# Self-attention of a channel-attention layer: diagonal chunk pairs computed on and above the diagonal only, the rest mirrored like other pairs

## The chip, the cores and the metric

The kernel runs on one core of a Trainium2 chip, and the metric is the device time of one execution in microseconds (us). An execution was profiled besides; its span runs from its first to its last instruction. The engines are called by their names in the profile: PE (TensorE), ACT (ScalarE), DVE (VectorE), POOL (GpSimd) and SP (SyncE, which here only issues DMAs).

## The reference, cut to what matters

`x` has shape 4 x 32 x 128 x 128, all in float32. Layer 0 regroups each image to 128 channels at 64 x 64 = 4096 tokens and lets the 4096 tokens of each image attend to one another, by cosine similarity of their 128 channels:

```python
q = xs.reshape(B, C * R * R, hw)                       # 4 x 128 x 4096
energy = jnp.einsum('bci,bcj->bij', q, q)              # 4096 x 4096, symmetric
d = jnp.sqrt(jnp.diagonal(energy, axis1=1, axis2=2))
energy = energy / (d[:, :, None] * d[:, None, :])
attn = jax.nn.softmax(energy, axis=-1)
out = jnp.einsum('bcj,bij->bci', q, attn)
out = gamma * out + xs
```

Layer 1 takes the result as tokens of 128 features: a layer norm, a linear attention without softmax over 8 heads, a residual; then a layer norm, a router over 8 experts of which the two best are mixed, and a residual.

What matters here is that the energy, and so its exponential before the division by the row sums, is symmetric: block (i, j) of exp(energy) is the transpose of block (j, i).

## The kernel before, in words

**Tiling of layer 0.** The 4096 tokens of an image are cut into 8 chunks of 512 (`NCH`), and each chunk into 4 blocks of 128 (`NJ`). `qn[i]` is chunk i of the normalised q (128 channels x 512 tokens), `qT[i]` the same chunk of q with tokens on the partitions. `attend` (line 207) loops over the chunks i (a *row* below, lines 213 to 251) and in it over the chunk pairs (i, jc) with jc up to i (line 221); a pair has 4 steps, j = 0 to 3. Thus an image has 36 pairs, of which 8 are diagonal (jc = i), and 144 steps. Only pairs on and below the diagonal of chunks are computed; the mirrored ones come by transposition.

**A step** (lines 225 to 240): PE computes 128 x 512 energies into the PSUM tile `pe` (line 228); ACT takes the exponential into `pr`, with its row sum into `sums` (line 230); PE adds the previous step's values to `po`, the output of chunk i (`values`, line 219, one step late); DVE transposes the 32 x 32 squares of `pr` into `F`, when the pair is not diagonal (line 234).

**The end of a pair that is not diagonal** (lines 241 to 247): the squares are in place but still have to go to the partitions of their mirrored block. Sixteen DMAs, from SBUF to SBUF, one for each of 4 x 4 groups of 32 partitions, take `F` to `G` (line 246). All are issued by SP. Then `transposed_share` (line 189) is put on the list `late`: 4 units, of which each is a matmul of `G` into `pg` (line 193) and an ACT copy of `G` that only serves its row sum (line 198); the last unit adds `pg` to `o[jc]`, the output of chunk jc (line 204). A unit is taken from the list at a step, not before 4 steps after the pair's end (`LAG`), one share after the other.

**A diagonal pair** computes all of its 4 x 4 blocks directly, and has no `F`, no `G` and no share.

**Buffers** that set how far one engine may run ahead of another: `pe` 2, `pr` 6, `F` 2, `G` 3, `po` 1, `pg` 1.

**Side work.** `prep` (line 144) loads a part of an image (`xx`), transposes and normalises it. `layer1` (line 259) carries layer 1 of an image; it loads `x` again as `T`, divides by the row sums (`den`, line 283), adds on POOL (line 335), and so on until the output DMAs (line 518). The loop at the end (lines 532 to 553) spreads these over the steps of `attend`: image 0 has only `prep` and the weights beside it; images 1 to 3 have layer 1 of the image before, from step 9 to step 138, and `prep` of the next near their end. Layer 1 of the last image runs alone at the end.

**What sets the order.** The loops give the order of the program. A scheduler in the kernel's framework then orders each engine's instructions by this order and by when it expects their inputs to be ready, so that for instance the four `pg` matmuls of a share may stand together, and places the waits. Each engine, and SP's queue, works through its own list in order. SP's list holds the loads of `xx` and `T` (line 141), the sixteen `G<-F` DMAs of each pair and the output DMAs.

Of the kernel before, what the change touches and what calls it, by code (L numbers as in the profile page):

```python
# [9 lines left out]
F32 = mybir.dt.float32  # L10
BF16 = mybir.dt.bfloat16
AF = mybir.ActivationFunctionType
ALU = mybir.AluOpType
# [5 lines left out]
def kernel(  # L19
# [10 lines left out]
    expert_b: bass.AP,  # L30
    out: bass.AP,
):

# [16 lines left out]
    nc = tc.nc  # L52
    P = 128
    B, C, H, W = x.shape
    N = (H // 2) * (W // 2)
    NB = N // P
    CH = 512
    NCH = N // CH
    NJ = CH // P
    HW2 = W // 2  # L60
    KT = 32
    S = 32
# [12 lines left out]
    work = ctx.enter_context(tc.tile_pool(name="work", bufs=2))  # L75
    stat = ctx.enter_context(tc.tile_pool(name="stat", bufs=2))
# [111 lines left out]

    def transposed_share(b, st, i, jc, G):

        pg = ps_g.tile([P, CH], F32, tag="pg", name=f"pg_{b}_{i}_{jc}")
        for ib in range(NJ):
            nc.tensor.matmul(  # L193
                pg, st["qT"][i][:, ib, :], G[:, ib].rearrange("p a j -> p (a j)"),
                start=(ib == 0), stop=(ib == NJ - 1),
            )
            junk = work.tile([P, CH], BF16, tag="junk", name=f"junk_{b}_{i}_{jc}_{ib}")
            nc.scalar.activation(  # L198
                junk, G[:, ib].rearrange("p a j -> p (a j)"), AF.Copy,
                accum_out=st["sums"][:, NJ * i + ib, jc : jc + 1],  # L200
            )
            if ib == NJ - 1:
                o = st["o"][jc].rearrange("p (j a c) -> p a j c", a=4, c=S)
                nc.vector.tensor_tensor(o, o, pg.rearrange("p (a j c) -> p a j c", a=4, c=S), ALU.add)  # L204
            yield "done" if ib == NJ - 1 else None

    def attend(b, st):

        qT, qn = st.setdefault("qT", {}), st.setdefault("qn", {})
        st["sums"] = sums = stat.tile([P, NB, NCH], F32, tag="sums", name=f"sums_{b}")  # L210
        st["o"] = []

        for i in range(NCH):
            po = ps_o.tile([P, CH], F32, tag="po", name=f"po_{b}_{i}")
            pend = None

            def values(pend, i=i, po=po):
                pr, t = pend
                nc.tensor.matmul(po, qT[t // NJ][:, t % NJ, :], pr, start=(t == 0), stop=(t == NJ * (i + 1) - 1))  # L219

            for jc in range(i + 1):
                off = jc < i
                if off:
                    F = fpool.tile([P, CH // S, NJ, S], F32, tag="F", name=f"F_{b}_{i}_{jc}")
                for j in range(NJ):
                    t = NJ * jc + j
                    pe = ps_e.tile([P, CH], F32, tag="pe", name=f"pe_{b}_{i}_{t}")
                    nc.tensor.matmul(pe, qn[jc][:, ts(j, P)], qn[i], start=True, stop=True)  # L228
                    pr = ppool.tile([P, CH], F32, tag="pr", name=f"pr_{b}_{i}_{t}")
                    nc.scalar.activation(pr, pe, AF.Exp, accum_out=sums[:, t, i : i + 1])  # L230
                    if pend is not None:
                        values(pend)
                    if off:
                        nc.vector.transpose(F[:, :, j, :], pr)  # L234
                    pend = (pr, t)
                    clock[0] += 1
                    if late and late[0][0] <= clock[0]:
                        if next(late[0][1], "done") == "done":
                            late.pop(0)
                    yield  # L240
                if off:
                    G = gpool.tile([P, NJ, 4, P], F32, tag="G", name=f"G_{b}_{i}_{jc}")
                    blocks = F.rearrange("p (ib q) j c -> p q ib (j c)", q=4)
                    for a in range(4):
                        for q in range(4):
                            nc.sync.dma_start(G[ts(q, S), :, a, :], blocks[ts(a, S), q])  # L246
                    late.append((clock[0] + LAG, transposed_share(b, st, i, jc, G)))
            values(pend)
            o = opool.tile([P, CH], F32, tag="o", name=f"o_{b}_{i}")
            nc.vector.tensor_copy(o, po)  # L250
            st["o"].append(o)
# [280 lines left out]
    for b in range(B):  # L532
        streams = []
        if b == 0:
            for kc, begin, end in ((1, 0, 8), (2, 10, 26), (3, 30, 60)):
                streams.append((prep(0, kc, states[0]), begin, end, 9))
            streams.append((setup_weights(), 60, 70, 3))
        else:
            p = states[b - 1]
            work_left = layer1(b - 1, p, False)  # L540
            streams.append((work_left, 9, 138, SIDE))
        if b + 1 < B:
            for kc, at in enumerate((96, 121, 128, 134)):
                streams.append((prep(b + 1, kc, states[b + 1]), at, at + 9, 9))
        done = [0] * len(streams)
        for t, _ in enumerate(attend(b, states[b])):
            for n, (steps, begin, end, count) in enumerate(streams):
                while t >= begin and done[n] * (end - begin) < (t + 1 - begin) * count:
                    next(steps, None)
                    done[n] += 1  # L550
        for steps, *_ in streams:
            for _ in steps:
                pass
    finish_late()
    last = states[B - 1]
# [40 lines left out]
```

## Time and profile before

| | us |
|---|---|
| three runs | 1920.04, 1922.54, 1923.35 |
| median | 1922.54 |
| the profiled execution's own time | 1923.41 |
| its span | 1921.4 |
| first `pe` matmul of image 0, 1, 2, 3, from the span's start | 19.7, 381.4, 852.0, 1306.7 |
| last `G<-F` issue | 1753.0 |

A line of the costliest groups reads: line, engine, operation, out<-in by the program's names, shapes, count, then busy time and mean ns of one, then the idle time of the engine before these and what ended most of it. A float32 matmul shows as two records. A line of the timeline reads: start, duration, engine, line, operation, tiles, count of like instructions in a row. SP's records are the times for which the issue of a DMA held its queue. A line of SP's waits reads: who waited for whom, us in total, times, longest. Image 0 lasts from 19.7 to about 381 and has little side work; in images 1 to 3 the first rows, 0 to 2, have little as well.

### The profile page before, as it was taken

The numbers are of one execution on the slowest core, as the hardware profiler recorded it, in microseconds if no ns is written. First come the engines' busy times: TensorE is split into PE (matmuls) and PEld (weight loads), VectorE is DVE, ScalarE is ACT, GpSimd is POOL, SyncE is SP. The second block draws the span as 40 slices with busy tenths as digits, with TensorE's granted clock in tenths as the row PEclk, the third lists the DMA queues.
The fourth block names the chain that finished last, engine by engine and source line by source line (L and its number), as shares of the span: only waits on it lengthen the run. The fifth ranks groups of instructions, "written<-read, shape, count | busy, mean of one in ns | idle before, by whom it ended". The sixth has DMA issues, their size and how long they took to land.

```text
span 1921.4 us, 20402 instructions
## 1 busy us (share of the span) xinstructions
PE 1845.2 (96%) x5320; PEld 897.6 (47%) x5320; DVE 880.0 (46%) x2029; ACT 959.0 (50%) x2925; POOL 293.0 (15%) x275
## 2 busy tenths in 40 slices
PE   6999999999999999999999999999999999996787
PEld 3444444444555444444555444444555444443643
DVE  3333333444335454645344454653534544444456
ACT  2444444445564454554665545454556454543544
POOL 0000000012000121212010122220200012211235
PEclk9999999999999999999999999999999999998879
DMA  5333343341333232344232233334222323234001
GB/s 118 77 88 75 88 102 92 97 88 47 74 78 85 64 84 74 82 96 88 65 89 70 68 81 79 80 85 94 65 62 70 86 66 86 63 87 93 1 12 33
DMA packets 314274, 145.63 MB, mean 76 GB/s; under 512 B 32528, under 2 KB 314160, under 8 KB 314160
## 3 DMA queue, kind: packets, MB, share of 16 engines
q1 hardware_dynamic: 310528, 142.73, 31.3%
q10 hardware_dynamic: 3632, 1.60, 0.4%
q8 instruction: 44, 0.72, 0.2%
q14 instruction: 70, 0.57, 0.1%
HBM read 18.38 MB, written 8.39 MB: 14 GB/s over the span
## 4 chain that ended last, share of the span: by engine, by line
PE 85%; DVE 5%; POOL 4%; ACT 3%; DMA 2%; SPq 1%; issue 1%; ACTq 0%; POOLq 0%; DVEq 0%
PE po L219 24%; PE pe L228 23%; PE pg L193 19%; PE py L505 5%; PE py L498 5%; PE pl L419 2%; PE pat L400 1%; PE pbe L488 1%; DVE df L327 1%; POOL T L335 1%; ACT xn L310 1%; PE ptn L179 1%; ACT tmp L507 1%; PE pgram L353 1%; SPq L246 1%
## 5 line engine op out<-in xcount | busy, mean ns | idle before, releaser
L230 ACT ACTIVATE pr<-pe 128x512 f32<-128x512 f32 x576 | 343.7, 597 | 600.7 <-PE pe L228 593.2
L219 PE MATMUL po<-pr,qT 128*128 128x512 f32 x1152 | 589.9, 595 | 3.2 <-ACT pr L230 1.9
L234 DVE STREAM_TRANSPOSE F<-pr 128x512 f32<-128x512 f32 x448 | 308.6, 703 | 337.4 <-ACT pr L230 304.5
L228 PE MATMUL pe<-qn,qn 128*128 128x512 f32 x896 | 456.6, 594 | 0.2
L193 PE MATMUL pg<-G,qT 128*128 128x512 f32 x896 | 422.6, 597 | 2.6 <-DMA G<-F 2.6
L219 PEld LDWEIGHTS po<-pr,qT 128*128 128x128 f32 x1152 | 213.9, 190 | 275.4 <-issue 232.5
L198 ACT ACTIVATE junk<-G 128x512 bf16<-128x512 f32 x448 | 276.2, 624 | 3.7 <-DMA G<-F 3.7
L193 PEld LDWEIGHTS pg<-G,qT 128*128 128x128 f32 x896 | 170.6, 192 | 214.0 <-issue 209.7
L507 ACT ACTIVATE tmp<-py,gate 128x128 f32<-128x128 f32 x512 | 146.4, 370 | 180.3 <-PE py L505 156.8
L228 PEld LDWEIGHTS pe<-qn,qn 128*128 128x128 f32 x896 | 160.9, 191 | 159.6 <-issue 157.8
L500 DVE SCALAR_TENSOR_TENSOR acc<-py,gate,acc 128x128 f32<-128x128 f32 x512 | 175.5, 349 | 107.6 <-PE py L498 94.2
L511 POOL TENSOR_TENSOR tmp<-tmp 128x512 f32<-128x512 f32 x64 | 81.6, 1275 | 620.3 <-ACT tmp L507 620.3
L204 DVE TENSOR_TENSOR o<-o,pg 128x512 f32<-128x512 f32 x112 | 76.7, 685 | 213.9 <-PE pg L193 213.0
L505 PE MATMUL py<-ew_sb,xn 128*128 128x512 f32 x256 | 133.1, 606 | 4.4 <-ACT tmp L507 4.4
L498 PE MATMUL py<-ew_sb,xn 128*128 128x512 f32 x256 | 130.5, 595 | 2.6 <-DVE acc L500 2.3
L228 PE MATMUL pe<-qn 128*128 128x512 f32 x256 | 131.6, 597 | 0.0
L230 ACT ACTIVATION_READ_ACCUMULATOR pr<-pe 128x1 f32 x576 | 114.2, 198 | 0.0
L105 POOL TENSOR_TENSOR rn<-ss,neg_half 128x8 f32<-128x8 f32 x16 | 26.3, 1642 | 463.8 <-DVE ss L169 463.8
L198 ACT ACTIVATION_READ_ACCUMULATOR junk<-G 128x1 f32 x448 | 87.9, 196 | 0.0
L505 PEld LDWEIGHTS py<-ew_sb,xn 128*128 128x128 f32 x256 | 48.5, 193 | 67.0 <-issue 42.2
L498 PEld LDWEIGHTS py<-ew_sb,xn 128*128 128x128 f32 x256 | 47.6, 191 | 63.1 <-issue 38.9
L310 ACT ACTIVATE xn<-T,nb_a,rs_a 128x128 f32<-128x128 f32 x128 | 51.2, 480 | 40.9 <-DVE nb_a L306 40.8
(99 smaller groups left out, 1213.3 us busy)
## 6 DMA issues: line engine op xcount, KB each, us to landing
G<-F SPq DMA_DIRECT2D x1792, 64.0 KB, 2.1
xx<-in_x_dram SPq DMA_DIRECT2D x64, 128.0 KB, 3.0
T<-in_x_dram SPq DMA_DIRECT2D x16, 512.0 KB, 5.7
out_dram<-acc SPq DMA_DIRECT2D x128, 64.0 KB, 1.8
ew_sb<-in_L_ffn_expert_w_dram ACTq DMA_DIRECT2D x1, 512.0 KB, 5.5
raw_w<-in_L_attn_Wv_dram ACTq DMA_DIRECT2D x1, 512.0 KB
raw_w<-in_L_attn_Wk_dram ACTq DMA_DIRECT2D x1, 256.0 KB
raw_w<-in_L_attn_Wq_dram ACTq DMA_DIRECT2D x1, 256.0 KB
```

Of the source, the lines that this page charges most:

```text
L193: nc.tensor.matmul(pg, st["qT"][i][:, ib, :], G[:, ib].rearrange("p a j -> p (a j)"), start=(ib == 0), stop=(ib == NJ - 1),)
L198: nc.scalar.activation(junk, G[:, ib].rearrange("p a j -> p (a j)"), AF.Copy, accum_out=st["sums"][:, NJ * i + ib, jc : jc + 1],)
L204: nc.vector.tensor_tensor(o, o, pg.rearrange("p (a j c) -> p a j c", a=4, c=S), ALU.add)
L219: nc.tensor.matmul(po, qT[t // NJ][:, t % NJ, :], pr, start=(t == 0), stop=(t == NJ * (i + 1) - 1))
L228: nc.tensor.matmul(pe, qn[jc][:, ts(j, P)], qn[i], start=True, stop=True)
L230: nc.scalar.activation(pr, pe, AF.Exp, accum_out=sums[:, t, i : i + 1])
L234: nc.vector.transpose(F[:, :, j, :], pr)
L498: nc.tensor.matmul(py, xn[:, k, :], ew_sb[:, 0:4, :], start=True, stop=True)
L500: nc.vector.scalar_tensor_tensor(acc[:, j, :], py[:, ts(e, D)], gate[:, k, e : e + 1], acc[:, j, :], ALU.mult, ALU.add)
L505: nc.tensor.matmul(py, xn[:, k, :], ew_sb[:, 4:8, :], start=True, stop=True)
L507: nc.scalar.activation(tmp[:, jk, e, :], py[:, ts(e, D)], AF.Copy, scale=gate[:, k, 4 + e : 5 + e])
L511: nc.gpsimd.tensor_tensor(tmp[:, :, 0:2], tmp[:, :, 0:2], tmp[:, :, 2:4], ALU.add)
```

## The change

In a diagonal pair, step j computes only the columns from block j on, `c0 = 128 j`: pe and po have 512, 384, 256 and 128 columns, and so has the exponential. The six blocks below the diagonal are mirrored from those above as in other pairs: DVE transposes the columns above the diagonal of steps 0 to 2 into `F` (384, 384 and 256 columns; one block on the diagonal is taken along), POOL sets one block of `F` to zero that the DMAs read and nobody writes, SP issues 16 DMAs with 3 rows of 96 values for each of 32 partitions, where other pairs have 4 rows of 128, and a share of 3 units follows, with `pg` matmuls of 384, 256 and 128 columns. Its row sums go to a ninth column of `sums`, which POOL sets to zero once an image. The last diagonal pair of the last image stays as it was (`full`), so that 31 of the 32 are changed. A few blank lines are left out of the diff.

```diff
@@ -188,26 +189,32 @@
 
     def transposed_share(b, st, i, jc, G):
 
+
+
         pg = ps_g.tile([P, CH], F32, tag="pg", name=f"pg_{b}_{i}_{jc}")
-        for ib in range(NJ):
-            nc.tensor.matmul(
-                pg, st["qT"][i][:, ib, :], G[:, ib].rearrange("p a j -> p (a j)"),
-                start=(ib == 0), stop=(ib == NJ - 1),
+        pgv = pg.rearrange("p (a f) -> p a f", a=4)
+        blocks = [(ib, P) for ib in range(NJ)] if jc < i else [(ib, S * ib) for ib in range(NJ - 1, 0, -1)]
+        for n, (ib, w) in enumerate(blocks):
+            last = n == len(blocks) - 1
+            src = G[:, ib, :, :w]
+            nc.tensor.matmul(pgv[:, :, :w], st["qT"][i][:, ib, :], src, start=(n == 0), stop=last)
+            junk = work.tile([P, 4, P], BF16, tag="junk", name=f"junk_{b}_{i}_{jc}_{ib}")
+            col = jc if jc < i else NCH
+            nc.scalar.activation(
+                junk[:, :, :w], src, AF.Copy, accum_out=st["sums"][:, NJ * i + ib, col : col + 1]
             )
-            junk = work.tile([P, CH], BF16, tag="junk", name=f"junk_{b}_{i}_{jc}_{ib}")
-            nc.scalar.activation(
-                junk, G[:, ib].rearrange("p a j -> p (a j)"), AF.Copy,
-                accum_out=st["sums"][:, NJ * i + ib, jc : jc + 1],
-            )
-            if ib == NJ - 1:
-                o = st["o"][jc].rearrange("p (j a c) -> p a j c", a=4, c=S)
-                nc.vector.tensor_tensor(o, o, pg.rearrange("p (a j c) -> p a j c", a=4, c=S), ALU.add)
-            yield "done" if ib == NJ - 1 else None
+            if last:
+                nj = blocks[0][1] // S
+                o = st["o"][jc].rearrange("p (j a c) -> p a j c", a=4, c=S)[:, :, :nj]
+                add = pg.rearrange("p (a j c) -> p a j c", a=4, c=S)[:, :, :nj]
+                nc.vector.tensor_tensor(o, o, add, ALU.add)
+            yield "done" if last else None
 
     def attend(b, st):
 
         qT, qn = st.setdefault("qT", {}), st.setdefault("qn", {})
-        st["sums"] = sums = stat.tile([P, NB, NCH], F32, tag="sums", name=f"sums_{b}")
+        st["sums"] = sums = stat.tile([P, NB, NCH + 1], F32, tag="sums", name=f"sums_{b}")
+        nc.gpsimd.memset(sums[:, :, NCH:], 0.0)
         st["o"] = []
 
         for i in range(NCH):
@@ -215,35 +222,46 @@
             pend = None
 
             def values(pend, i=i, po=po):
-                pr, t = pend
-                nc.tensor.matmul(po, qT[t // NJ][:, t % NJ, :], pr, start=(t == 0), stop=(t == NJ * (i + 1) - 1))
+                pr, t, c0 = pend
+                nc.tensor.matmul(
+                    po[:, c0:], qT[t // NJ][:, t % NJ, :], pr[:, c0:], start=(t == 0), stop=(t == NJ * (i + 1) - 1)
+                )
 
             for jc in range(i + 1):
-                off = jc < i
-                if off:
+                within = jc == i
+                full = within and b == B - 1 and i == NCH - 1
+                if not full:
                     F = fpool.tile([P, CH // S, NJ, S], F32, tag="F", name=f"F_{b}_{i}_{jc}")
                 for j in range(NJ):
                     t = NJ * jc + j
+                    c0 = P * j if within and not full else 0
                     pe = ps_e.tile([P, CH], F32, tag="pe", name=f"pe_{b}_{i}_{t}")
-                    nc.tensor.matmul(pe, qn[jc][:, ts(j, P)], qn[i], start=True, stop=True)
+                    nc.tensor.matmul(pe[:, c0:], qn[jc][:, ts(j, P)], qn[i][:, c0:], start=True, stop=True)
                     pr = ppool.tile([P, CH], F32, tag="pr", name=f"pr_{b}_{i}_{t}")
-                    nc.scalar.activation(pr, pe, AF.Exp, accum_out=sums[:, t, i : i + 1])
+                    nc.scalar.activation(pr[:, c0:], pe[:, c0:], AF.Exp, accum_out=sums[:, t, i : i + 1])
                     if pend is not None:
                         values(pend)
-                    if off:
+                    if not within:
                         nc.vector.transpose(F[:, :, j, :], pr)
-                    pend = (pr, t)
+                    elif not full and j < NJ - 1:
+                        c1 = max(c0, P)
+                        nc.vector.transpose(F[:, c1 // S :, j, :], pr[:, c1:])
+                    pend = (pr, t, c0)
                     clock[0] += 1
                     if late and late[0][0] <= clock[0]:
                         if next(late[0][1], "done") == "done":
                             late.pop(0)
                     yield
-                if off:
+                if not full:
                     G = gpool.tile([P, NJ, 4, P], F32, tag="G", name=f"G_{b}_{i}_{jc}")
                     blocks = F.rearrange("p (ib q) j c -> p q ib (j c)", q=4)
+                    ib0, w = 0, P
+                    if within:
+                        nc.gpsimd.memset(F[:, 4:8, 2, :], 0.0)
+                        ib0, w = 1, 3 * S
                     for a in range(4):
                         for q in range(4):
-                            nc.sync.dma_start(G[ts(q, S), :, a, :], blocks[ts(a, S), q])
+                            nc.sync.dma_start(G[ts(q, S), ib0:, a, :w], blocks[ts(a, S), q, ib0:, :w])
                     late.append((clock[0] + LAG, transposed_share(b, st, i, jc, G)))
             values(pend)
             o = opool.tile([P, CH], F32, tag="o", name=f"o_{b}_{i}")
```

## The prediction

> **What bounds the kernel now.** I read the page first (engine shares, the chain that ended last, the costliest groups), then TensorE's timeline, then SP's own queue.
>
> ```profile
> PE 1845.2 (96%) x5320; PEld 897.6 (47%) x5320; DVE 880.0 (46%) x2029; ACT 959.0 (50%) x2925; POOL 293.0 (15%) x275
> ...
> PE 85%; DVE 5%; POOL 4%; ACT 3%; DMA 2%; SPq 1%; issue 1%; ACTq 0%; POOLq 0%; DVEq 0%
> ...
> L219 PE MATMUL po<-pr,qT 128*128 128x512 f32 x1152 | 589.9, 595 | 3.2 <-ACT pr L230 1.9
> L228 PE MATMUL pe<-qn,qn 128*128 128x512 f32 x896 | 456.6, 594 | 0.2
> L193 PE MATMUL pg<-G,qT 128*128 128x512 f32 x896 | 422.6, 597 | 2.6 <-DMA G<-F 2.6
> ```
>
> TensorE is busy nearly throughout, the chain runs through it, and it loses some 6 us in all before its three main groups. The timeline gives the true price of a matmul, since the starts are real and the ends modelled. Here is TensorE inside a diagonal pair, and, from elsewhere, 128-column matmuls:
>
> ```profile
> 726.83 1.02 PE L228 MATMUL pe<-qn 128*128 128x512 f32 x2
> 727.69 1.02 PE L219 MATMUL po<-pr,qT 128*128 128x512 f32 x2
> 728.55 1.02 PE L193 MATMUL pg<-G,qT 128*128 128x512 f32 x2
> ```
> ```profile
> 1010.55 1.05 PE L400 MATMUL pat<-mat,xnT 128*128 128x128 f32 x8
> ```
>
> A 512-column matmul is two records and takes 0.86 us from start to start. The eight `pat` records are four matmuls of 128 columns; the next matmul starts at 1011.44, so one takes 0.22 us, a quarter. Narrow matmuls really are cheap.
>
> Then SP's queue, which the busy shares leave out: how long one issue holds it, how it looks in image 0, and how long it waits there (window 38 to 394).
>
> ```profile
> L246 SPq DMA_DIRECT2D G<-F x1792: 585/599/2023, 37.9 to 1753.0; - x200
> ```
> ```profile
> 295.75 30.96 SPq L246 DMA_DIRECT2D G<-F  x48
> 326.75 2.10 SPq L141 DMA_DIRECT2D xx<-in_x_dram  x4
> ```
> ```profile
> SPq L246 <- DVE F L234: 58.4, 9, 11.1
> ```
>
> One issue holds SP for 0.6 us, and 48 in a row take 30.96 us: 0.645 us each, 10.3 us for the 16 of a pair. With the occasional 2 us issue the 112 groups average 10.5 us plus 0.1 us to the next: **10.6 us of SP a pair**. An off-diagonal pair without side work costs TensorE 12 x 0.86 = 10.3 us. So inside a row SP is the slower of the two already, and it catches up in the diagonal pair, where today it has nothing to do. Those are the waits of the last line.
>
> **What the Trainium skill says.** "FP8 and Floating Point Precision", TensorE Precision Notes: true FP32 takes four passes through the array. The trace agrees: at the 2.4 GHz of "TensorE: Matmul & The Clock Gate", 4 x 512 columns are 0.853 us, and 0.86 is seen. The latter page, LDWEIGHTS: loading 128 weight columns takes about 107 ns whatever the rows, which would floor narrow matmuls; the `pat` records lie 0.111 us apart, so 128 columns just hide their load. "Perfetto Trace Analysis", Summary: the profiler window per engine type: a DMA's record on its issuing queue is lock wait, descriptor generation and semaphore, not the movement. Hence the 0.6 us is the queue's own time; the trace agrees, as the data lands at 2.1 us while the next issue has long started. "DMA: Bandwidth & Descriptors", Issuing engines are not separate DMA queues: issue time is "usually small relative to the DMA itself". Not here: 16 issues, 10.3 us, against 2.1 us.
>
> **The change, part by part** (31 diagonal pairs: 8 in each image, less the last of the last).
>
> TensorE. Before: 8 x 0.86 = 6.87 us a pair. After, widths 512, 384, 256, 128 for pe and again for po: 0.86 + 0.645 + 0.43 + 0.22 = 2.15 us, twice, 4.31; pg of 384, 256, 128: 1.29. Together 5.60: 1.27 us saved a pair, **39.4 us over 31**, if TensorE stays the bound. Widths 384 and 256 are not shown; I take them in proportion. They cannot exceed 0.86 or fall under 0.22; only a mean far above proportion would matter, and the 128-column row speaks against it.
>
> ScalarE and VectorE. ScalarE: four exps of 1280 columns instead of 2048, three copies with a sum more, and three reads of the accumulator. From 597 ns at 512 columns and 370 at 128 (L507), exps 1.94, copies 1.42, reads 7 x 0.2: 4.75 against 3.18 us, 1.6 more. VectorE: three transposes and an add, at most 3 x 0.70 + 0.69 = 2.8 us more. That is 49 and 87 us in the run on engines at 50 and 46%: hidden under TensorE and SP. If that cover went, it would be these sums.
>
> GpSimd. A memset a diagonal pair, about 0.18 us (L394's takes 176 ns), and one an image. The 16 DMAs wait for it, and behind them on SP the next groups and loads. It can sit behind one T add (2.35 us) in GpSimd's queue. Between nothing and 2.4 us, taken at nothing: it is due after the pair's last transpose, and SP is then behind anyway.
>
> SP. 16 more DMAs a pair, 96 rows of 384 bytes instead of 128 of 512. **Not shown, so bounded:** the quickest write of the output took 0.315 us (median 0.446, also 128 rows), the T loads with 1024 rows 0.594, G<-F with 128 rows 0.599. Issue time hardly follows the row count, so I take the like operation, 10.6 us a group; low end 0.49 us with the gap, 7.9 us; 31 groups are 329 us. SP waits on F for 407 us in the whole run, so it fits on average. It doesn't fit where the waits are short, and new groups stand ahead of the xx, T and output DMAs.
>
> Image 0. From (1,0)'s group at 37.94 to (7,6)'s at 383.86 there are 346 us; 27 groups take 286 and 16 loads 8.5, leaving 51 free. Into this go (1,1) to (6,6), 6 x 10.6 = 64, and (0,0)'s end, 1 us. **SP comes 14 us late** to (7,6), at 397.5.
>
> Start of image 1. From there to (3,0)'s group lie (7,6), (7,7), (0,0), (1,0), (1,1), (2,0), (2,1), (2,2), 8 x 10.6, and T's four loads, 2.5: it starts at 484.8, not at 466.8. How far can TensorE run ahead? F has two buffers, pr six. Before, the exps of (3,0) ended at 449.3, 17.5 us ahead of SP; counting buffers (a group blocked, its successor's transposes after landing) I get 13. I take 15: exps at 469.8, **20.5 us later than before**. Then side work makes rows slower than SP, and five diagonal pairs save 5 x 1.27 = 6.4: +14.1 on leaving image 1.
>
> Image 2. (7,6) ended at 853.4, now 867.5; seven groups and T, 76.7 us, put (3,0) at 944.2, exps at 929.2 against 911.1: +18.1, less 6.4: +11.7. Image 3 the same way, from 1308.6 and 1365.8: 1308.6 + 11.7 + 76.7 - 15 - 1365.8 = +16.2, less four pairs, 5.1: +11.1. The last image's final pair and tail are unchanged. **Sum:** the profiled execution, 1923.4 us (span 1921.4 and 2.0 around it), plus 11.1 is 1934.5; the median lies 0.9 lower: **1934 us**. All 39 us of TensorE turn into waiting for SP. A lead of 13 or 17 us gives about 6 more or less; with a few us less in image 0 the case spans 1915 to 1950.
>
> **Rivals.**
> - **The narrow DMAs are issued quickly** (ends faster). The point that decides is 51 / 6 = 8.5 us a group, 0.53 an issue. At 7.9 us image 0 takes 47 of its 51 us, and the start of image 2 needs 4 x 7.9 + 3 x 10.6 + 2.5 = 66 of the 66.3 us from 853.4 to 919.7. Then TensorE's 39.4 come through: 1884, some 1888 with small stalls. For it: the output's 0.446. Against: the like operation never fell under 0.585. 0.20.
> - **SP cannot be filled.** Transposes come in the order the program was scheduled in, and in image 0 SP stood idle for 7.9 us after (6,4) though (6,5)'s exps were done at 277.5 (issue 295.8). If a third of the 51 us stays unused, 17 us more are carried through, and with a lead of 13 us 6 more: 1957. 0.25.
> - **A wait on the memset or on late T loads** holds GpSimd and the first layer-1 steps in each image: 31 x 0.5 us on top: 1950. 0.05.
>
> **How the numbers follow.** My case 0.50 (0.05 of it faster, 0.10 same, 0.35 slower), the quick issue 0.20 (0.19 faster, 0.01 same), the unfilled queue 0.25 and the memset 0.05 (slower). Over 0.2%, 3.8 us, about what a measurement of this kernel can tell from no change: faster 0.24, same 0.11, slower 0.65. The range, 1898 to 1964, leaves out most of the quick issue and the end of the unfilled queue. Most of the chance lies on the slow side.
>
> **What would show it.** Right: 2288 G issues near 0.6 us; in image 0 SP's wait for F nearly gone, SP's issues back to back; TensorE with idle time in image 0 and at the start of each image; pe, po and pg records of 128 columns near 0.11 us apart. Wrong: issues of the narrow form well under 0.53 us, TensorE without gaps, image 1 beginning earlier than 381.

## The result

| | before | after |
|---|---|---|
| median of four runs, us | 1922.94 (1920.04 to 1924.67) | 2105.65 (2104.91 to 2106.65) |
| profiled execution: time, span | 1923.41, 1921.4 | 2105.97, 2104.2 |
| TensorE's mean granted clock | 0.983 | 0.948 |

The ratio is 1.095 (95% interval 1.093 to 1.097): **183 us slower**. I had forecast 1934 us, within 1898 to 1964. The direction is right, the size is not, and only the 21 us of image 0 were lost in the way that I had forecast.

In the kernel after, `pg` is line 200, `po` 226, `pe` 239, the exponential 241, the transposes 245 (diagonal pairs 248), the memset 260 and the `G<-F` issue 264. Its page first: busy shares, chain, two of the costliest groups.

```profile
PE 1885.5 (90%) x5506; PEld 947.7 (45%) x5506; DVE 895.4 (43%) x2153; ACT 967.1 (46%) x3111; POOL 298.6 (14%) x310
...
PE 58%; SPq 19%; DVE 8%; POOL 4%; DMA 4%; issue 3%; ACT 3%; ACTq 0%; POOLq 0%; DVEq 0%
...
L226 PE MATMUL po<-pr,qT 128*128 128x512 f32 (+3 forms) x1152 | 550.0, 562 | 9.0 <-ACT pr L241 8.0
...
L200 PE MATMUL pg<-G,qT 128*128 128x512 f32 (+2 forms) x1082 | 473.7, 581 | 21.8 <-DMA G<-F 10.6
```

TensorE has 39 us less to do, and yet its busy time rose by 40 us: ends are modelled, and matmuls ran at half the clock more often. In the chain SP's queue went from 1% to 19%, TensorE fell from 85% to 58%. The three main groups wait only some 25 us more (`po` 9.0 us, `pg` 21.8, `pe` 0.0). So the loss has to be looked for elsewhere, and the first cut is by image. Here and below an image runs from its first exponential to the first of the next, the last one to its last exponential; the rest is the tail.

| us | image 0 | image 1 | image 2 | image 3 | tail |
|---|---|---|---|---|---|
| before | 360.7 | 470.6 | 454.7 | 443.6 | 170.0 |
| after | 381.5 | 515.2 | 518.9 | 485.2 | 181.5 |
| difference | +20.8 | +44.6 | +64.2 | +41.6 | +11.5 |

**Image 0 is what the prediction described.** SP's issues in the kernel after (first the form of all of them: count, then min/median/max in ns), a stretch of SP's timeline, and the longest of SP's waits between 38 and 400 us (who waited for whom, us in total, times, longest):

```profile
L264 SPq DMA_DIRECT2D G<-F x2288: 585/599/2716, 26.9 to 1936.8; - x191
```
```profile
286.99 58.45 SPq L264 DMA_DIRECT2D G<-F  x88
```
```profile
SPq L264 <- PE pe L239: 3.7, 10, 0.5
```

The narrow issue costs what the wide one does, SP issues 88 in a row without a pause, and its wait for F, 58 us before, is gone from the list. (7,6)'s group starts at 399.4, where I had 397.5.

**Images 1 to 3 are not.** SP is not full there: from 415 to 910 us it waits 82 us for F. Still, its issues hold 18.5% and 21.2% of the chain in images 1 and 2, where before they are not among the chain's 18 largest parts; so SP's load is not out as a cause yet. TensorE waits, and for side work. Its longest waits in images 1 to 3 (engine, line, releaser, us in total, times, longest), before (window 382 to 1751) and then after (403 to 1922):

```profile
PE pgram L353 <- ACT xn L310: 3.5, 2, 2.8
...
PE ptn L179 <- DVE qs L176: 1.2, 1, 1.2
```
```profile
PE pbd L341 <- DVE df L345: 24.5, 6, 9.0
PE ptn L180 <- DVE qs L177: 24.2, 9, 6.3
PE pgram L371 <- ACT xn L328: 23.7, 6, 4.3
```

In these three images TensorE is idle 118 us longer than before, and 68 us of this are these three waits. They belong to `prep` and layer 1, which the change does not touch. Here is one of them in row 7 of image 1: TensorE, VectorE, GpSimd, SP.

```profile
898.89 0.81 PE L239 MATMUL pe<-qn 128*128 128x384 f32 x2
899.53 1.02 PE L226 MATMUL po<-pr,qT 128*128 128x512 f32 x2
900.39 0.59 PE L239 MATMUL pe<-qn 128*128 128x256 f32 x2
900.82 0.81 PE L226 MATMUL po<-pr,qT 128*128 128x384 f32 x2
901.47 0.38 PE L239 MATMUL pe<-qn 128*128 128x128 f32 x2
901.69 1.12 PE L158 MATMUL ptq<-ident,xx 128*128 128x128 f32 x8
909.15 1.94 PE L180 MATMUL ptn<-ident,qs 128*128 128x128 f32 x8 [6.34 <-DVE qs L177]
910.88 5.21 PE L200 MATMUL pg<-G,qT 128*128 128x512 f32 x8
```
```profile
905.87 0.69 DVE L170 TENSOR_REDUCE ss<-sq 128x4 f32<-128x512 f32 x1
908.31 1.29 DVE L177 TENSOR_TENSOR qs<-qT,rn 128x512 f32<-128x512 f32 x2 [1.76 <-POOL rn L106]
909.52 2.48 DVE L245 STREAM_TRANSPOSE F<-pr 128x512 f32<-128x512 f32 x4
```
```profile
906.63 1.65 POOL L106 TENSOR_TENSOR rn<-ss,neg_half 128x8 f32<-128x8 f32 x1 [15.45 <-DVE ss L170]
```
```profile
902.44 2.02 SPq L536 DMA_DIRECT2D out_dram<-acc  x4
912.07 8.33 SPq L264 DMA_DIRECT2D G<-F  x13
```

The first six lines also show the narrow matmuls as priced: 0.64 us at 384 columns, 0.43 at 256, 0.22 at 128. Then `ptn` waits for the chain `ptq`, `ss`, `rn`, `qs`, and nothing stands between. Work was there: the `pg` behind `ptn` needs pair (7,4), whose issues had ended at 889.8. The transposes of (7,6) stand behind `qs`, although their exponentials ended at 893.8; so they come 16 us late, and SP idles from 904.5 to 912.1. No engine is short of time here. The **order of the lists** is bad. In the kernel before, a chain of the same kind in the same row has nine `pe`, `po` and `pg` matmuls in between, back to back (first and last of them):

```profile
832.85 1.11 PE L157 MATMUL ptq<-ident,xx 128*128 128x128 f32 x8
833.80 1.02 PE L219 MATMUL po<-pr,qT 128*128 128x512 f32 x2
...
840.67 1.02 PE L219 MATMUL po<-pr,qT 128*128 128x512 f32 x2
841.53 0.60 PE L179 MATMUL ptn<-ident,qs 128*128 128x128 f32 x4
```

The waits cost twice. The four `pg` matmuls at 910.88 take 5.05 us to the next start (915.93) instead of 4 x 0.86 = 3.44: the granted clock is 0.50 until 914.1. By image (length, busy times, then PEclk, DMA share, GB/s), image 1 and 2 before and after:

```profile
382.50:853.10 470.60, 464.56 (x1357) 225.37 (x1356) 227.44 (x519) 245.21 (x750) 75.12 (x66) 1.00 0.32 76
853.10:1307.80 454.70, 452.50 (x1325) 219.89 (x1324) 220.39 (x506) 239.41 (x732) 73.44 (x65) 1.00 0.33 79
```
```profile
403.40:918.60 515.20, 470.67 (x1373) 236.15 (x1373) 224.10 (x539) 241.25 (x780) 74.82 (x74) 0.95 0.33 79
918.60:1437.50 518.90, 470.53 (x1373) 236.16 (x1372) 224.10 (x539) 241.16 (x780) 74.80 (x74) 0.94 0.33 79
```

A mean clock lower by 0.05 over 515 us and by 0.06 over 519 us is worth some 26 and 31 us at full clock. Part of that falls in time in which TensorE waits anyway: counted from the trace's clock records, it is busy at half the clock for some 40 us in each of the two images, and so loses some 20 us that no list of waits shows.

**My theory** after this: 16 more issues a pair fill SP in image 0; in images 1 to 3 they make the scheduler order the lists so that the chains of side work have no cover, even where the real SP has room. **Rivals:** the memset, which waits for F's buffer at the head of GpSimd's list (241 us in total) and holds up `rn`, `rs` and the T adds; the added shares or narrow matmuls themselves; and SP's real load in all images.

### The profile page after: what moved, and what is told of

Same layout as the page of the kernel before. It is cut to its first block, busy times and chain, and to the rows that moved or that the text cites. A ratio compares the mean times of both kernels' runs of the same rounds, so it can differ in the third digit from the quotient of the medians.

```text
span 2104.2 us, 22221 instructions
## 1 busy us (share of the span) xinstructions
PE 1885.5 (90%) x5506; PEld 947.7 (45%) x5506; DVE 895.4 (43%) x2153; ACT 967.1 (46%) x3111; POOL 298.6 (14%) x310
## 3 DMA queue, kind: packets, MB, share of 16 engines
q1 hardware_dynamic: 366080, 161.05, 32.3%
## 4 chain that ended last, share of the span: by engine, by line
PE 58%; SPq 19%; DVE 8%; POOL 4%; DMA 4%; issue 3%; ACT 3%; ACTq 0%; POOLq 0%; DVEq 0%
SPq L264 18%; PE pg L200 15%; PE po L226 14%; PE pe L239 14%; PE py L523 4%; PE py L516 4%; DMA G<-F 2%; DMA T<-in_x_dram 2%; DVE F L245 1%; PE pbe L506 1%; ACT tmp L525 1%; POOL T L353 1%; PE pl L437 1%; DVE df L345 1%; PE pgram L371 1%
## 5 line engine op out<-in xcount | busy, mean ns | idle before, releaser
L226 PE MATMUL po<-pr,qT 128*128 128x512 f32 (+3 forms) x1152 | 550.0, 562 | 9.0 <-ACT pr L241 8.0
L241 ACT ACTIVATE pr<-pe 128x512 f32<-128x512 f32 (+1 forms) x576 | 320.2, 558 | 499.7 <-PE pe L239 487.8
L200 PE MATMUL pg<-G,qT 128*128 128x512 f32 (+2 forms) x1082 | 473.7, 581 | 21.8 <-DMA G<-F 10.6
L203 ACT ACTIVATE junk<-G 128x512 bf16<-128x512 f32 (+3 forms) x541 | 313.2, 586 | 72.1 <-DMA G<-F 43.8
L245 DVE STREAM_TRANSPOSE F<-pr 128x512 f32<-128x512 f32 x448 | 281.0, 681 | 130.2 <-DMA G<-F 122.0
L200 PEld LDWEIGHTS pg<-G,qT 128*128 128x128 f32 x1082 | 212.4, 201 | 261.0 <-issue 245.9
L210 DVE TENSOR_TENSOR o<-o,pg 128x512 f32<-128x512 f32 (+1 forms) x143 | 93.9, 656 | 465.5 <-PE pg L200 465.3
L523 PE MATMUL py<-ew_sb,xn 128*128 128x512 f32 x256 | 138.8, 629 | 15.8 <-DVE acc L518 8.8
L516 PE MATMUL py<-ew_sb,xn 128*128 128x512 f32 x256 | 136.4, 619 | 14.7 <-ACT tmp L525 11.1
L203 ACT ACTIVATION_READ_ACCUMULATOR junk<-G 128x1 f32 x541 | 105.0, 194 | 0.0
L239 PE MATMUL pe<-qn 128*128 128x512 f32 (+3 forms) x256 | 92.1, 444 | 0.0
```

Source lines behind the costliest of these rows:

```text
L200: nc.tensor.matmul(pgv[:, :, :w], st["qT"][i][:, ib, :], src, start=(n == 0), stop=last)
L203: nc.scalar.activation(junk[:, :, :w], src, AF.Copy, accum_out=st["sums"][:, NJ * i + ib, col : col + 1])
L210: nc.vector.tensor_tensor(o, o, add, ALU.add)
L226: nc.tensor.matmul(po[:, c0:], qT[t // NJ][:, t % NJ, :], pr[:, c0:], start=(t == 0), stop=(t == NJ * (i + 1) - 1))
L239: nc.tensor.matmul(pe[:, c0:], qn[jc][:, ts(j, P)], qn[i][:, c0:], start=True, stop=True)
L241: nc.scalar.activation(pr[:, c0:], pe[:, c0:], AF.Exp, accum_out=sums[:, t, i : i + 1])
```

## The experiments

The first column is the time in us: of one run for memset, transport and narrow, for both lists in order, for after with one list in order, diagonal issues on ScalarE and diagonal pairs over HBM; the median of four in the others. The kernel before ran beside them at 1922.9 to 1925.9. The lengths by image come from each kernel's profiled execution:

| kernel | time | image 0 | 1 | 2 | 3 | tail |
|---|---|---|---|---|---|---|
| before | 1922.9 | 360.7 | 470.6 | 454.7 | 443.6 | 170.0 |
| after | 2105.7 | 381.5 | 515.2 | 518.9 | 485.2 | 181.5 |
| memset on VectorE | 2107.6 | 379.9 | 515.0 | 518.9 | 487.2 | 182.9 |
| transport only | 2132.2 | 382.3 | 525.2 | 525.8 | 495.6 | 179.8 |
| narrow only | 1864.1 | 335.6 | 457.8 | 443.8 | 435.2 | 168.4 |
| image 0 only | 1944.6 | 381.0 | 470.9 | 454.9 | 443.6 | 170.5 |
| late rows only | 2009.7 | 361.1 | 490.3 | 491.5 | 461.0 | 181.7 |
| before, both lists in order | 2007.9 | 382.4 | 484.4 | 481.3 | 459.7 | 176.7 |
| after, both lists in order | 2061.7 | 414.1 | 486.8 | 491.5 | 465.8 | 180.2 |
| after, TensorE's in order | 2091.6 | 412.6 | 499.6 | 505.5 | 475.1 | 175.4 |
| after, VectorE's in order | 2027.9 | 385.6 | 475.5 | 481.0 | 465.8 | 196.3 |
| before, VectorE's in order | 1966.1 | 375.1 | 468.7 | 468.8 | 452.0 | 183.4 |
| late rows, VectorE's in order | 1980.8 | 375.9 | 459.4 | 469.0 | 456.8 | 196.4 |
| diagonal issues on ScalarE | 2055.7 | 411.8 | 482.5 | 490.9 | 477.0 | 170.7 |
| after, 4 of 16 on ScalarE | 1938.7 | 376.9 | 469.1 | 458.1 | 447.1 | 162.6 |
| before, 4 of 16 on ScalarE | 1941.8 | 369.0 | 465.0 | 465.9 | 453.3 | 163.3 |
| diagonal pairs over HBM | 1995.4 | 380.5 | 477.8 | 481.8 | 458.0 | 173.7 |
| TensorE mirrors | 1936.2 | 370.5 | 474.7 | 454.3 | 443.1 | 170.2 |

### Which part costs the time

**Memset on VectorE.** `nc.gpsimd.memset(F[:, 4:8, 2, :], 0.0)` becomes `nc.vector.memset(...)`.

> The kernel after, with the zeroing of F's one block on VectorE instead of GpSimd; TensorE's, ScalarE's and SP's lists of instructions stay in the order of the kernel after. Theory of the order (16 more issues of 0.6 us a diagonal pair fill SP in image 0, and the list of each engine, made for a fuller SP, leaves the chains of side work without cover in images 1 to 3): 2095 to 2110 us, the GpSimd waits for F's buffer (241 us) gone, the stalls of TensorE before ptn, pgram and py still there. Theory of the memset (it waits for F's buffer at the head of GpSimd's queue and holds pow and the T adds behind it): under 2000 us, as these stalls, some 40 us an image with the halved clock after them, go.

2107.6. GpSimd's wait for F's buffer is gone, TensorE's three waits in images 1 to 3 are the same to about 1 us (window 401 to 1922):

```profile
PE pbd L341 <- DVE df L345: 25.6, 6, 9.3
PE ptn L180 <- DVE qs L177: 24.1, 9, 6.3
PE pgram L371 <- ACT xn L328: 23.8, 6, 4.3
```

The memset is refuted: 241 us of waiting that nobody waited for.

**Narrow matmuls only.** F, G and the share stay as they were, for pairs off the diagonal alone (`if not within:` in place of `if not full:`); the blocks below the diagonal are left out.

> Only the narrow pe, exp and po of the diagonal pairs: no transposes into F, no memset, no DMAs and no share for them, so that the blocks below the diagonal are left out of the sums and of the output in all 32 diagonal pairs. TensorE does 12 matmuls of 512 columns fewer by 6.87 - 4.31 = 2.56 us a pair. Theory of SP and order: 1923 - 32 x 2.56 = 1841, so 1835 to 1855 us, without gaps on TensorE. Theory that narrow matmuls cost more than in proportion, or break TensorE's pace: 1900 us or more.

1864.1, 9 us above the expected range, since images 1 to 3 save 8 to 13 us where TensorE's work falls by 20. Still, the narrow forms are no cost. The run also gives an estimate of what the change could bring if its transport cost nothing: with the mirrored `pg` added, 31 x 1.29 = 40 us, some 1904 us, 1% less than before.

**Transport only.**

```diff
-                    c0 = P * j if within and not full else 0
+                    c0 = 0
...
-                    late.append((clock[0] + LAG, transposed_share(b, st, i, jc, G)))
+                    if not within:
+                        late.append((clock[0] + LAG, transposed_share(b, st, i, jc, G)))
```

> The diagonal pairs computed in full as before, and besides the transposes into F, the memset and the 16 DMAs of the change, into a G that nobody reads; no share for them. So TensorE and ScalarE do the work of the kernel before and the output is that of the kernel before; only the transport is added. Theory of SP and order: the loss is all here, 2080 to 2160 us (the kernel after has 2105.7 with 39 us less of TensorE work). If the loss comes with the added shares or the narrow matmuls: 1922 to 1940 us.

2132.2. All of the loss is here, image by image; no share and no narrow matmul is needed for it. The kernel after, with its 39 us less for TensorE, is 26 us faster than this one.

### Which pairs

**Image 0 only,** and **late rows only** (`full` is made true for the other diagonal pairs):

```diff
-                full = within and b == B - 1 and i == NCH - 1
+                full = within and b > 0
```
```diff
-                full = within and b == B - 1 and i == NCH - 1
+                full = within and (b == 0 or i < 3 or b == B - 1 and i == NCH - 1)
```

> The change only in the 8 diagonal pairs of image 0; images 1 to 3 as in the kernel before. Theory of SP as in the prediction: image 1 starts 14 to 21 us late, as it did after the change, and rows 0 to 2 of image 1 have three issue groups fewer than after; a late SP queue of 14 us at (7,6) against a lead of 15 us: 1923 + 10 to 25, so 1933 to 1950 us. If a late SP queue in image 0 is what disturbs the later images too (stalls of 40 to 60 us an image there): 2000 us or more.

> The change only in the diagonal pairs of rows 3 to 7 of images 1 to 3 (14 pairs; the last one of the last image stays full); image 0 and rows 0 to 2 as in the kernel before. These are the rows in which SP has room: in the kernel before it waits there more than the 10.6 us that a group takes. My prediction's model: each saves 1.27 us of TensorE, 1923 - 18 = 1905 us. Theory of the order (the lists, made for a fuller SP, leave the side work's chains without cover even where the real SP has room): slower than before, 1940 to 2040 us, with stalls before ptn, pgram, pbd, py in images 1 to 3.

Image 0 only: 1944.6, ratio 1.011 (1.009 to 1.013). Image 0 is 20.3 us longer, images 1 to 3 are within 0.3 us of the kernel before. So the late SP queue of image 0 costs its 20 us once and disturbs nothing after. Late rows: 2009.7, 1.045 (1.043 to 1.047). Fourteen pairs, where my model had a gain of 18 us, lose 86. SP has room there: it waits 191 us for F from 382 to 1345 us. This is the run that fells the prediction.

### Is it the order

In the next kernels each instruction of an engine is pinned behind the one traced before it, so that its list has the order of the program; where TensorE's list is among the pinned, a share comes 6 steps after the pair's end.

```diff
+            return lambda *a, **k: tc.keep_in_program_order(getattr(self.engine, name)(*a, **k))
...
-    LAG = 4
+    LAG = 6
```

> The kernel after, with TensorE's and VectorE's lists in the order of the program instead of the scheduler's, and shares 6 steps after the pair's end instead of 4. Theory of the order: the stalls in images 1 to 3 go for the most part, as a pe, a po and a pg stand between any two steps of side work: images 1 and 2 at 450 to 480 us instead of 515 and 519; image 0 stays late (SP is really full there), 380 to 400. Theory that SP's real load alone makes the loss: images 1 and 2 stay at 510 us or more.

> The same two edits on the kernel before: TensorE and VectorE in the order of the program, shares after 6 steps. The control: image by image it says what the program's order itself costs (between 0 and 10 per cent, I have no number for it), and with the run before it what the change is worth when both have the same order: theory of the order, images 1 and 2 of the two differ by under 15 us; theory that SP's real load alone makes the loss, by 45 to 65 us as with the scheduler's order.

> The kernel after with only TensorE's list in the order of the program, shares after 6 steps; VectorE's list by the scheduler. If TensorE's list carries the loss of images 1 to 3 (prep and layer-1 matmuls and pg placed where nothing covers them): images 1 and 2 near 483 and 484 us, as with both lists. If VectorE's list does (transposes behind waiting side work): 500 us or more each.

> The kernel after with only VectorE's list in the order of the program; TensorE's by the scheduler, shares after 4 steps. If VectorE's list carries the loss: images 1 and 2 near 483 us; if TensorE's list does: 500 us or more each.

The program's order is no good order, 85 us worse for the kernel before. But with both lists in this order in both kernels, images 1 to 3 lose 2, 10 and 6 us to the change, not 45, 64 and 42. These controls leave TensorE idle more than the kernel before (22.7 us in image 1 instead of 6.0), and some cost of the change can hide in that. The change is not free with the lists pinned either: 54 us are left (2061.7 against 2007.9), 32 of them in image 0. (Images 1 and 2 at 487 and 492 are a little over the 450 to 480 expected, image 0 at 414 is over the 380 to 400. The last two expectations' 483 and 484 counted an image from an exponential a few steps too early; counted as in the table they are 487 and 492.) The plainest comparison needs no control: in the kernel after, with the same issues on SP, VectorE's list alone brings images 1 to 3 back by 40, 38 and 19 us, TensorE's alone by 16, 13 and 10. So most of the loss lies in VectorE's list; I take it that TensorE's follows it, as the scheduler still sets that one to fit. With VectorE in order the wait before `ptn`, over the whole run 42.4 us in the kernel after, has all but gone; another, there 32.3, has grown:

```profile
PE pgram L380 <- ACT xn L337: 49.4, 12, 10.8
...
PE ptn L189 <- DVE qs L60: 6.3, 1, 6.3
```

**Late rows once more,** with VectorE in order, and its control:

> The kernel before with only VectorE's list in the order of the program: the control for the run of the kernel after with this edit (2028 us) and for the next kernel. With both lists in order the kernel before took 2008 us; I expect 1950 to 2000 us here.

> The change only in rows 3 to 7 of images 1 to 3 (14 pairs, where SP has room), with VectorE's list in the order of the program. My prediction had a saving of 1.27 us a pair here, 18 us; with the scheduler's order it was a loss of 86 us. Theory that the order alone made that loss: 5 to 25 us faster than the kernel before with the same edit. Theory that the groups on SP cost time there whatever the order: 10 us slower than it or more.

1980.8 against 1966.1, ratios to the kernel before 1.030 (1.028 to 1.032) and 1.023 (1.021 to 1.025). So 15 are left of the 86 us that late rows cost, once VectorE's list has the program's order in both kernels; 71 hang on that list. But the gain that I expected is not there either; 15 us slower is what I had put down for groups on SP that cost time there whatever the order. (With all 31 pairs changed and VectorE's list in order, 62 us are left: 2027.9 against 1966.1.) In the profiled executions, which differ by 10 us, image 1 saves 9.3 us, image 2 nothing, image 3 loses 4.8, and the tail is 13.0 longer. In the tail it can be seen: SP's last `G<-F` issue comes 15.8 us after the last exponential, in the control 2.4. The last pairs' transport reaches into the tail. Where the rest went I did not settle.

### Is it SP's issues that make the order

**Diagonal issues on ScalarE:** `(nc.scalar if within else nc.sync).dma_start(...)`; **4 of 16 on ScalarE** in all pairs, in the kernel after and in the kernel before: `(nc.scalar if a == 3 else nc.sync).dma_start(...)`.

> The kernel after, with the 16 DMAs of each diagonal pair issued by ScalarE's queue instead of SP's. Theory of SP: SP has the load of the kernel before again, ScalarE gets 496 x 0.6 = 298 us of issue on top of some 1010 us, so 1880 to 1950 us. Theory of the memset: nothing changes at GpSimd, about 2100 us. Theory that the narrow matmuls or the added shares themselves cost the time: about 2100 us.

> The kernel after, with 4 of the 16 issues of every pair (those of the last 32 partitions of F) on ScalarE's queue, so that SP has 12: 143 x 12 = 1716 issues on SP, fewer than the 1792 of the kernel before, and 572 on ScalarE, 4 x 0.6 = 2.4 us a pair. Theory that the fullness of SP's queue makes both the late image 0 and the poor order: image 0 below 360 us, images 1 to 3 within 10 us of the kernel before, 1884 to 1925 us. If ScalarE's exps are held up by issues that wait for the transposes ahead of them in its queue, as with 16 at once (2056 us): 1950 us or more, with TensorE waiting for pr at po.

> The kernel before with the same split, the control: SP was hardly a bound there, so within 10 us of 1923 us if the issues on ScalarE cost its exps nothing that TensorE sees; 1940 us or more if they hold up the exps.

Sixteen at once: 2055.7, between the expectations and inconclusive. Against the kernel after, images 1 to 3 gain 33, 28 and 8 us, and image 0 loses 30. Exponentials now stand in ScalarE's list behind issues that wait for transposes, and over the whole run `po` waits 46.5 us for them. But in image 0 that is only 9.2 us, and its longest wait is `ptn`'s, 20.3; its loss is not settled. Four in every pair: **1938.7**, 1.008 (1.007 to 1.010), with its control at 1941.8, 1.010 (1.008 to 1.012), where `po` waits 30.0 us for exponentials, as its second case had it; between these two the change is worth 3 us, not 39. Images 1 to 3 of the kernel after are back at 469.1, 458.1 and 447.1, though the scheduler is free and transposes, memset, shares and transfers are the change's. What differs is where the issues stand: 1716 in SP's list instead of 2288, and 572 in ScalarE's. This lightens SP's real load too, so the time alone does not say which of the two mattered. The lists do, since they are made before the kernel runs, and they can be read from the traces. `prep` makes four parts for the next image during image 1 and four during image 2; the table counts the `pe`, `po` and `pg` matmuls on TensorE from a part's last `ptq` to its first `ptn`. In these kernels the counts are the same in both images:

| kernel | matmuls in between, four parts |
|---|---|
| before; image 0 only; narrow only; TensorE mirrors (below) | 11, 11, 12, 9 |
| after; memset on VectorE | 2, 3, 0, 9 |
| late rows only | 2, 3, 0, 7 |
| transport only | 2, 4, 1, 7 |
| 4 of 16 on ScalarE, after and before | 11, 12, 12, 10 |
| diagonal issues on ScalarE | 50, 12, 12, 8 |

The cover is thin in just those kernels that have the added issues of images 1 and 2 in SP's list, and back when they stand elsewhere. That is the best evidence that their number makes the order. Why image 0 missed its "below 360" is shown in part: ScalarE waits there 51.9 us before exponentials for issues of its own, and TensorE waits 10.0 us at `po` for exponentials, but 13.1 us before `ptn` too (window 22 to 398):

```profile
ACT pr L241 <- DMA G<-F: 51.9, 15, 4.5
```
```profile
PE ptn L180 <- DVE qs L177: 13.1, 6, 3.4
PE po L226 <- ACT pr L241: 10.0, 11, 1.4
```

**Over HBM.** A pair's F goes out in 1 DMA and comes back in 4. Some lines:

```diff
+                        D = dpool.tile([P, 4, 3 * P], F32, tag="D", name=f"D_{b}_{i}_{jc}")
+                        nc.sync.dma_start(D, F.rearrange("p x j c -> p (x j c)").rearrange("p (q n) -> p q n", q=4)[:, :, P:])
+                        for a in range(4):
+                            nc.sync.dma_start(
+                                G[:, a, 1:, :].rearrange("p ib f -> p (ib f)"), D[ts(a, S)].rearrange("p q n -> q p n")
+                            )
```

> The kernel after, but F goes to G of a diagonal pair over a scratch in HBM: 1 DMA out and 4 back, 5 issues instead of 16 (some zeroed blocks go along); other pairs as they are. The transposes, the memset (larger), F, G and the share stay. Theory of SP: 5 x 0.6 = 3 us of issue, and perhaps 2 to 3 us of SP waiting for the first DMA to land, against 10.6: image 0 then needs 6 x 6 = 36 of its 51 free us, and the time falls to 1885 to 1940 us. If F's and G's buffers, the transposes or the added share cost the time rather than SP's issues: 2050 us or more.

> As the kernel after, with the hop over HBM in all pairs: 5 issues a pair everywhere. Theory of SP: SP is at about half its load of the kernel before, no image start is late, TensorE's 39 us come through: 1880 to 1900 us. The other way: the hop's two landings (2 to 3 us each) and 1 MB more through HBM a pair delay every pg, 1930 us or more.

> The kernel before (diagonal pairs in full) with the hop over HBM in all its pairs. It says what the hop alone does: theory of SP: SP was not the bound before, so within 1 per cent of 1923 us, perhaps 10 us less as TensorE's few stalls at pg go; if the hop's latency hurts: over 1940 us.

Diagonal pairs alone: 1995.4, 110 us better than after and short of the 1885 to 1940. Images 1 to 3 lose 7, 27 and 14 us (the counts of the table are 12, 12, 6 and 9 or 10 here); image 0 gains nothing. SP, which issues both ways, stands still for landings. In image 0 (window 21 to 402) it does so before other pairs' issues, until a `G<-D` has landed, and before a way back, until its `D<-F` has:

```profile
SPq L273 <- DMA G<-D: 22.6, 17, 1.8
SPq L267 <- DMA D<-F: 15.1, 7, 2.2
```

In all pairs: 2759.5 and, without the change, 2680.9, ratios 1.435 and 1.393. A clear miss for both. In the one without the change SP waits 587 us for the first landings, and TensorE 473 us for the second ones at `pg`; in the one with it 752 and 549. Why TensorE's list has `pg` so early there was not followed up.

### A way without transport

**TensorE mirrors:** in the kernel before, narrow `pe`, exponential and `po`; the six blocks by TensorE transposes of `pr`, a ScalarE copy with the row sum and a `po` matmul from it.

```diff
+                for j in range(ib):
+                    nc.tensor.transpose(pt[:, ts(j, P)], prs[j][:, ts(ib, P)], ident)
+                nc.scalar.activation(m[:, :w], pt[:, :w], AF.Copy, accum_out=sums[:, NJ * i + ib, NCH : NCH + 1])
...
+                nc.tensor.matmul(po[:, : P * ib], qT[i][:, ib, :], m[:, : P * ib], start=False, stop=(ib == NJ - 1))
```

> The kernel before with narrow pe, exp and po in all 32 diagonal pairs; the six blocks below the diagonal come by TensorE transposes into PSUM and a ScalarE copy with the row sum, so SP has no issue more than in the kernel before. TensorE per pair: 4.31 us of narrow pe and po, six 128-column transposes 0.6 to 1.3 us, 1.29 us of mirrored po, 6.2 to 6.9 us against 6.87. Theory of SP and order: 1900 to 1925 us, no stalls like those of the kernel after. Theory that any mirroring inside a diagonal pair stalls TensorE (the wait for ScalarE's copy before the mirrored po): 1940 us or more.

1936.2, 1.007 (1.006 to 1.009), between the two expectations: images 1 to 3 are at the length of before or 4 us over, image 0 is 10 us over. Six transposes and waits eat what the narrow matmuls save; the wait of `po`'s weight loads for the copy is 10.4 us of it in the whole run. No version here that computes all blocks beats the kernel before.

## Why the prediction was wrong

1. **TensorE's saving:** right. Widths 384, 256 and 128 cost in proportion; the saving turns up where nothing swallows it (narrow only).
2. **ScalarE and VectorE hidden:** right for their busy time, and too large as sizes: it rose by 8 and 15 us, not 49 and 87. What did not stay hidden is the order of VectorE's list (7).
3. **The memset at nothing:** right, for its time. It waited 241 us, unseen.
4. **The narrow issue at 0.6 us:** right, 585/599. The rival of a quick issue is out.
5. **Image 0, 14 us late at (7,6):** right, 15.5; image 1 starts 20.9 us late, and the change in image 0 alone costs 21 us in all.
6. **Start of image 1:** already off. (3,0)'s group starts at 504.1, not at 484.8. I had SP back to back, but it waits 12 us for F, as (2,1)'s transposes come at 478.5, 30 us after its exponentials.
7. **The step that failed:** "Then side work makes rows slower than SP, and five diagonal pairs save 5 x 1.27 = 6.4." Room on SP was taken as enough, and every list was silently left in the order of before. The lists are made anew with each change. In these rows the change loses 86 us where I had 18 to gain (late rows only), and 71 of them go when VectorE's list has the program's order in both kernels.
8. **The halved clock** was not in the sum at all: some 20 us each in images 1 and 2, which had next to none before.
9. **The rival "SP cannot be filled"** named the kind, transposes in the scheduled order, but I looked for it in image 0, where SP's queue was full, and priced it at 17 + 6 us.

"PSUM — Partial Sum Buffer", Engine vs sequencer instructions, in the Trainium skill says that VectorE's queue is strict FIFO. The trace agrees, with the four transposes at 909.52 behind a `qs` that waits 1.76 us for GpSimd. It was the page that I should have set beside the sentence on SP's room.

What stays open: that the issues in SP's list change the order is shown by the lists, but how the scheduler reckons with SP was not looked at; where the 54 and 62 us come from that the change costs with pinned lists; and why late rows gain nothing in images 2 and 3 even with VectorE in order.

## What to carry to other kernels

More issues on a queue that has room by its sum are not free if a scheduler places other engines' work by what it expects of that queue. After a change, look first at what stands in the lists between a producer and its consumer in work that was not touched. Test with one part of the change in the rows where it should be harmless, and with the order pinned in both kernels, since the order is part of the change. And count a wait of TensorE of several microseconds with the slow clock behind it.

## What the runs showed of the hardware

- In the gap of 6.3 us before 909.15 the granted clock is halved. It is 1.00 from 902.8, where TensorE stops, to 907.3, and 0.50 from there to 914.1; from 915 on it is 1.00 again. "TensorE: Matmul & The Clock Gate", HAM oscillation — how this bites in real kernels, in the Trainium skill warns of idle gaps above some 3.4 us; this trace agrees.
- The issue of a DMA from F to HBM of 128 rows of 8 KB held SP for 0.344 us (median), one back of 2 KB rows for 0.528, where `G<-F` holds it for 0.599. So the price has a form-dependent part, though 96 rows of 384 bytes and 128 of 512 cost the same.
- With F going over HBM in all pairs of the kernel before, SP waited 587 / 105 = 5.6 us a time for the 1 MB of a pair to land in HBM before it could issue the way back.
